# One product for two blocks of sources in an attention layer: four places of one tile instead of four tiles

## Chip, cores and metric

The kernel runs on one core of a Trainium2 chip. The metric is the device time of one execution in microseconds (us), the median over several runs. It computes a two-layer graph attention network on 1250 nodes followed by a routed feed-forward layer, all of it in one launch.

## The reference, cut to what matters

```python
def gat_layer(x, W, att_src, att_dst, bias, src, dst, heads, out_ch, concat):
    h = (x @ W.T).reshape(n, heads, out_ch)
    a_src = jnp.einsum('nhc,hc->nh', h, att_src)
    a_dst = jnp.einsum('nhc,hc->nh', h, att_dst)
    e = jax.nn.leaky_relu(a_src[src] + a_dst[dst], 0.2)
    m = jax.ops.segment_max(e, dst, num_segments=n)
    ex = jnp.exp(e - m[dst])
    denom = jax.ops.segment_sum(ex, dst, num_segments=n)
    msg = (ex / (denom[dst] + EPS))[:, :, None] * h[src]
    out = jax.ops.segment_sum(msg, dst, num_segments=n)
    ...
x = x + gnn(layernorm(x))      # layer 1: 8 heads of 128 channels, relu; layer 2: 1 head of 768
x = x + ffn(layernorm(x))
```

There are 21250 edges between 1250 nodes. An edge can occur more than once. So the sum over edges can be written with dense matrices: for a head, the weight of a pair (source, destination) is exp(e - m) times the count of edges between the two, and the sum over sources is a matrix product of these weights with the rows of h.

## The kernel before, in words

**Blocks.** The 1250 nodes are ten blocks of 125 (B = 125, NB = 10). A first stage counts edges into the tile ct, 125 x 10 x 1250 in 16-bit integers: for each place in a block (the partition) and each block s of sources, the counts for all 1250 destinations. Then comes the first attention layer, the loop over h and s at L842 to L901, which holds the change. The projection of the second layer, the second attention (L1023) and the feed-forward part follow.

**One step (h, s) of the loop.** The function weights (L636) makes the weights of head h from source block s to all 1250 destinations, in a tile pt of 125 x 1250 floats:

- L640, on VectorE (DVE), *the begin*: the larger of (row 0 + a per-source number) and row 1. The two rows belong to the head and lie in the tile rows_h, which a DMA fills for each head.
- L643, on ScalarE (ACT), *the exponential*, in place.
- L644, on DVE, *the product*: the smaller of the exponential and 1, times the counts ct[:, s].

TensorE (PE) then multiplies the ten 125 x 125 pieces of pt with the rows of h (L863) and adds into four banks of accumulators, acc. One matmul on 32-bit floats is two instructions in the profile, so a step is 20. The tile pt has four buffers (`bufs=4`), so the begin of step s waits until PE has read step s - 4.

**What else lies in the loop.**

- *The tops* (L616, called through tops and top_steps, L717 to L723): for heads 5, 6 and 7, a running maximum over one block, on DVE, ten for a head. Heads 0 to 3 have four of them each in the source, heads 4 and 5 five, head 6 four, head 7 none. From head 4 on they are queued behind the product of their step (`tc.issue_after(formed.ins)`).
- *The rows of the next head* (load_destination_rows, L621, called at s = 5): small DVE operations (L624 to L628), a transposition on PE (L582), a copy on DVE (L584), a DMA out and a DMA that spreads the rows over all partitions (L631). The begins of head h + 1 wait for this DMA.
- *The end of the head before* (take, divide, turn): ACT copies the accumulators, DVE forms reciprocals (L741, L742), ACT divides, PE transposes.
- *Matmuls that fill PE*: in heads 0 and 1 the last of the first projection (L505), from head 2 on parts of the second projection (h2_part, L810). Their results go out through ACT or, for later parts, through a DVE addition (L818).

**What sets the order.** Each engine works through its own queue in order. The library that builds the program orders each queue from the dependencies and the order of the source, with its own estimates of durations; `issue_after` adds an edge. So the order in a queue is fixed before the run, and need not be that of the source.

The second attention layer uses the same function weights with 250 destinations at a time (weights2, L951).

Of the kernel before, what the change touches and what calls it, by code (L numbers as in the profile page):

```python
# [25 lines left out]
F32 = mybir.dt.float32  # L26
# [5 lines left out]
OP = mybir.AluOpType  # L32
AX = mybir.AxisListType

N = 1250
# [7 lines left out]
B = 125  # L43
NB = N // B
# [28 lines left out]
def gnn_ffn(  # L73
# [25 lines left out]
    nc = tc.nc  # L99

    def pool(name, bufs=1, space=None, stack=ctx):
        if space is None:
            return stack.enter_context(tc.tile_pool(name=name, bufs=bufs, reuse_waits="tile"))
        return stack.enter_context(tc.tile_pool(name=name, bufs=bufs, space=space))
# [7 lines left out]
    def ps_mm(name):  # L112
        return mm_pool[0].tile([128, 512], F32, tag="mm", name=name)

    def ps_tr(name):
        return psum.tile([128, 512], F32, tag="tr", bufs=2, name=name)
# [51 lines left out]
    def half_w(i, name):  # L168
        return big.tile([128, 4 * D], F32, tag="wa" if i == 0 else "wb", name=f"{name}{i}")
# [55 lines left out]
    ct = gpool.tile([B, NB, N], U16, name="ct")  # L225
# [363 lines left out]
    def low_high(a_s, shape, name):  # L589

        lo = const.tile(shape, F32, name=f"{name}_lo")
        nc.vector.tensor_scalar(lo, a_s, SLOPE, None, op0=OP.mult)
        hi = const.tile(shape, F32, name=f"{name}_hi")
        nc.vector.tensor_scalar(hi, a_s, 1.0 - SLOPE, None, op0=OP.mult)
        return lo, hi
# [7 lines left out]
    def load_source_row(hd, sp, row, name, to=None, tag="src_row", bufs=2):  # L603

        if to is None:
            to = sp.tile([128, N], F32, tag=tag, bufs=bufs, name=f"srow_{name}")
        nc.sync.dma_start(to, row.partition_broadcast(128))
        hd.src_row = to[:B]
# [24 lines left out]
        )  # L633
        hd.rows = t[:B]

    def weights(o, hd, lo, hi, s, c0, c1):  # L636

        begun = nc.vector.scalar_tensor_tensor(  # L640
            o, hd.rows[:, 0, c0:c1], hi, hd.rows[:, 1, c0:c1], op0=OP.add, op1=OP.max
        )
        nc.scalar.activation(o, o, AF.Exp, bias=lo, scale=1.0)  # L643
        formed = nc.vector.scalar_tensor_tensor(  # L644
            o, o, 1.0, ct[:, s, c0:c1], op0=OP.min, op1=OP.mult
        )
        return begun, formed


    heads = [Head() for _ in range(H1)]  # L650
# [25 lines left out]
    for b in range(4, NB):  # L676
# [9 lines left out]
        if b == 6:  # L686
            attention_columns()
            as1_lo, as1_hi = low_high(a1[:, 0], [B, H1, NB], "as1")
# [17 lines left out]
    ap = pool("attn", stack=attn)  # L706
# [20 lines left out]
    def take(h, acc):  # L727

        sums = ap.tile([B, NB, C1 + 1], F32, tag="sums", bufs=1, name=f"sums{h}")
        for g in range(NG):  # L730
            n = min(PER, NB - g * PER)
            act_copy(
                sums[:, g * PER : g * PER + n],
                acc[g][:B, : n * (C1 + 1)].rearrange("p (j c) -> p j c", j=n),
            )
        return sums

    def divide(h, sums):

        rec = ap.tile([B, NB], F32, tag="rec", bufs=2, name=f"rec{h}")  # L740
        nc.vector.tensor_scalar(rec, sums[:, :, C1], DEN_EPS, None, op0=OP.add)  # L741
        nc.vector.reciprocal(rec, rec)  # L742
        for d in range(NB):
            nc.scalar.activation(sums[:, d, :C1], sums[:, d, :C1], AF.Copy, scale=rec[:, d : d + 1])

    def turn(h, sums, g):

        n = min(PER, NB - g * PER)
        p = ps_tr(f"h1tp{h}_{g}")
        for j in range(n):  # L750
            nc.tensor.transpose(p[:, j * B : (j + 1) * B], sums[:, g * PER + j, :C1], ident[:B, :B])
        nc.scalar.activation(
            groups[h // 4][:, h % 4, g * PER * B : (g * PER + n) * B], p[:, : n * B],
            AF.Relu, bias=b1c[:, h : h + 1], scale=1.0,
        )
# [16 lines left out]
    def fold_att2(g, w2n):  # L772
        p = ps_tr(f"v2p{g}")
        for k in range(KD):
            for j in range(4):
                nc.tensor.matmul(
                    p[32 * j : 32 * j + 2, :128], att2c[:, k], w2n[:, k, j * 128 : (j + 1) * 128],
                    start=(k == 0), stop=(k == KD - 1),
                )
        v2_row = ap.tile([2, F1 // 2], F32, tag="v2_row", bufs=1, name=f"v2_row{g}")  # L780
        for j in range(4):
            act_copy(v2_row[:, j * C1 : (j + 1) * C1], p[32 * j : 32 * j + 2, :C1])
        v2_rows.append(v2_row)
# [16 lines left out]
    def load_w2(i):  # L800
        w2h.append(half_w(i, "w2s").rearrange("p (h f) -> p h f", h=4))
        nc.sync.dma_start(
            w2h[i], w2t[i * 512 : (i + 1) * 512].rearrange("(h p) f -> p h f", p=128)
        )
# [32 lines left out]
    h2_first = [(b, g) for b in range(NB) for g in range(2)]  # L837
    begun_in = {2: (5, 7, 9), 3: (4, 6, 7, 9)}
    late = []
    load_w2(0)  # L840
    todo = None
    for h in range(H1):  # L842
        hd = heads[h]
        acc = [ps_mm(f"acc{h}_{g}") for g in range(NG)]
        for s in range(NB):
            pt = ap.tile([B, N], F32, tag="pt", bufs=4, name=f"pt{h}_{s}")
            begun, formed = weights(
                pt, hd, as1_lo[:, h, s : s + 1], as1_hi[:, h, s : s + 1], s, 0, N
            )
            if s in top_steps.get(h, ()):  # L850
                if h < 4:
                    tops.pop(0)()
                else:
                    with tc.issue_after(formed.ins):
                        tops.pop(0)()
            if s == 0 and todo is not None:
                sums = take(*todo)
            if s == 1 and todo is not None:
                with tc.issue_after(begun.ins):
                    divide(todo[0], sums)  # L860
            for d in range(NB):
                g, j = divmod(d, PER)
                summed = nc.tensor.matmul(  # L863
                    acc[g][:B, j * (C1 + 1) : (j + 1) * (C1 + 1)],
                    pt[:, d * B : (d + 1) * B], h1v[h // 4][:, h % 4, s, :],
                    start=(s == 0 and j == 0), stop=(s == NB - 1), skip_group_check=True,
                )
            if s in (2, 3) and todo is not None:
                with tc.issue_after(summed.ins):
                    for g in (2 * s - 4, 2 * s - 3):  # L870
                        turn(todo[0], sums, g)
            if h in (4, 5) and s == 4:
                with tc.issue_after(formed.ins), tc.issue_after(summed.ins):
                    fold_att2(h - 4, w2n)
            if h in (4, 5) and s == 6:
                with tc.issue_after(formed.ins), tc.issue_after(summed.ins):
                    turn_att2(h - 4)
            if s == 5 and h + 1 < H1:
                load_destination_rows(heads[h + 1], ap, a1[:, 1, h + 1], f"h{h + 1}", 2)
            if s == 0 and h == 3:  # L880
                load_source_row(heads[7], ap, as1_d[7], "h7")
            if s in begun_in.get(h, ()):
                late.append((h2_first.pop(0), range(h, 4)))
                h2_part(0, *late[-1][0], range(h))
            if 4 <= h < H1 - 1 and s in ((2, 4, 6, 8) if h < 6 else (2, 5, 8)):
                h2_part(0, *h2_first.pop(0))
            if h == H1 - 1 and s in (1, 2, 3, 4, 5, 7, 8):
                at, hs = late.pop(0)
                h2_part(0, *at, hs)
            if h == H1 - 1 and s == 6:  # L890
                attention2(range(H1 - 1))
            if fill and s in (2, 4, 5, 7):
                fill.pop(0)()
        if h == 1:
            h2.append(big.tile([B, NB, D + 1], F32, tag="t", name="h2"))
            nc.gpsimd.memset(h2[0][:, :, D : D + 1], 1.0)
        if h in (3, 4):
            w2n = load_w2n(h - 3)
        if h == 5:
            load_w2(1)  # L900
        todo = h, acc  # L901
# [25 lines left out]
    as2_lo, as2_hi = low_high(a2[:, :, 0], [B, NB], "as2")  # L927
    hd = Head()
# [20 lines left out]
    pt2 = []  # L949

    def weights2(q):  # L951
        pt2.append(sp.tile([B, NB, 2 * B], F32, tag="pt2", bufs=3, name=f"pt2_{q}"))
        for s in range(NB):
            weights(
                pt2[q][:, s], hd, as2_lo[:, s : s + 1], as2_hi[:, s : s + 1], s,
                2 * q * B, 2 * (q + 1) * B,
            )

    for b in range(NB):
        for g in range(2):  # L960
# [62 lines left out]
    for q in range(NB // 2):  # L1023
        pt = pt2[q]
# [147 lines left out]
    pt = ps_tr("hidt")  # L1172
# [4 lines left out]
    pt = ps_tr("hidt4")  # L1177
# [15 lines left out]
    for r1, r0 in ((0, 3), (1, 4), (2, None)):  # L1193
        pair = [(1, r1)] if r0 is None else [(1, r1), (0, r0)]
        for m in range(KH):
            for r, a in pair:
                for g in range(2):
                    q = 32 * (2 * (1 - r) + g)
# [6 lines left out]
    for r in range(2):  # L1205
        for g in range(2):
            q = 32 * (2 * (1 - r) + g)
# [68 lines left out]
```

## Time and profile before

| | |
|---|---|
| median of 3 runs | 735.99 us (734.98 to 737.64) |
| the profiled execution | 735.11 us, its span 733.1 us |
| granted TensorE clock, mean | 0.993 |
| busy in the span | PE 95%, DVE 76%, ACT 40%, POOL 13% |
| L640 in the first layer | 80 of 125x1250, 118.6 us, 1511 ns each |
| L643 in the first layer | 80 of 125x1250, 105.7 us, 1336 ns each |
| L644 in the first layer | 80 of 125x1250, 114.7 us, 1452 ns each |
| L863, PE | 1600 instructions, 188.5 us |
| L616, DVE, all | 90, 130.7 us |

The span runs from the first to the last instruction that the profiler shows; the time of the execution has 2.0 us around it. The mean duration of an instruction (the column "mean ns") is longer than its step in a full queue, because the next one starts before the last is written off; the timeline gives the steps. "Idle before" is how long the engine stood still just ahead of an instruction, and the name behind the arrow is what ended that.

### The profile page before, as it was taken

How to read it: one execution, taken by the hardware profiler on the slowest of the kernel's cores; microseconds unless marked ns; L12 is line 12 of the kernel's file. 1: busy time of each engine (PE TensorE's matmuls, PEld its weight loads, DVE VectorE, ACT ScalarE, POOL GpSimd, SP SyncE). 2: the span in 40 equal slices, each digit the busy share in tenths (PEclk: the TensorE clock that was granted, in tenths of full speed). 3: DMA queues.
4: the chain of work that ended last, by engine and by line, in shares of the span. 5: the costliest groups of instructions: out<-in, count | busy, mean ns of one | idle time of the engine just before them, and what ended most of it. 6: DMA issues, size and time to landing. Idle time of an engine off the chain costs nothing.

```text
span 733.1 us, 10360 instructions
## 1 busy us (share of the span) xinstructions
PE 698.1 (95%) x4136; PEld 535.2 (73%) x4136; DVE 553.5 (76%) x943; ACT 289.9 (40%) x502; POOL 91.7 (13%) x95
## 2 busy tenths in 40 slices
PE   3899999999999989999999899999999999999997
PEld 3767888889898878888888776555555555676755
DVE  7989999889999999999999961879487222423212
ACT  5969621143563764847474734015044000010100
POOL 8449200000000000000000000000011010023110
PEclk9899999999999999999999999999999999999999
DMA  8445000340205012040401004022110100285711
GB/s 235 165 150 202 1 0 1 124 141 1 72 1 192 10 62 70 2 157 1 157 1 71 1 23 138 5 72 65 30 34 21 41 23 21 84 276 166 283 43 43
DMA packets 21701, 58.41 MB, mean 80 GB/s; under 512 B 2414, under 2 KB 7906, under 8 KB 20498
## 3 DMA queue, kind: packets, MB, share of 16 engines
q1 hardware_dynamic: 21598, 57.68, 23.7%
q8 instruction: 33, 0.54, 0.3%
q14 instruction: 18, 0.15, 0.1%
q10 hardware_dynamic: 52, 0.04, 0.0%
HBM read 53.74 MB, written 3.98 MB: 79 GB/s over the span
## 4 chain that ended last, share of the span: by engine, by line
PE 57%; DVE 33%; DMA 5%; issue 3%; ACT 1%; SPq 0%; DVEq 0%; ACTq 0%
PE acc L1033 16%; DVE pt L640 12%; DVE pt L644 10%; PE h2p L810 9%; PE h1p L505 8%; DVE unused L616 6%; PE f L1098 5%; PE f L1082 5%; PE acc L863 5%; DMA rows_h<-r_h_d 3%; PE count L302 3%; DVE ring L242 2%; PE xtp L397 1%; DMA r_h_d<-r_h_s 1%; PE xt2p L397 1%
## 5 line engine op out<-in xcount | busy, mean ns | idle before, releaser
L863 PEld LDWEIGHTS acc<-g,pt 125*125 125x125 f32 x1600 | 184.3, 189 | 25.5 <-DVE pt L644 18.5
L863 PE MATMUL acc<-g,pt 125*125 125x129 f32 x1600 | 188.5, 276 | 11.9 <-DVE pt L644 11.7
L643 ACT ACTIVATE pt<-pt,as_lo 125x1250 f32<-125x1250 f32 (+1 forms) x130 | 127.3, 1012 | 127.4 <-DVE pt L640 126.7
L644 DVE SCALAR_TENSOR_TENSOR pt<-pt,ct 125x1250 f32<-125x1250 f32 (+1 forms) x130 | 133.0, 1051 | 0.8 <-ACT pt L643 0.6
L1033 PE MATMUL acc<-h,pt 125*125 125x385 f32 (+1 forms) x400 | 129.7, 486 | 0.0
L640 DVE SCALAR_TENSOR_TENSOR pt<-rows_h,as_hi 125x1250 f32<-125x1250 f32 x80 | 118.6, 1511 | 2.3 <-DMA rows_h<-r_h_d 2.3
L1033 PEld LDWEIGHTS acc<-h,pt 125*125 125x125 f32 x400 | 74.6, 187 | 53.9
L810 PE MATMUL h2p<-w2s,g 128*125 128x384 f32 x320 | 110.7, 488 | 0.0
L505 PE MATMUL h1p<-w1s,xt 128*125 128x256 f32 x480 | 107.0, 380 | 0.8 <-ACT g L401 0.8
L505 PEld LDWEIGHTS h1p<-w1s,xt 128*125 128x125 f32 x480 | 88.9, 188 | 14.0 <-ACT g L401 1.2
L810 PEld LDWEIGHTS h2p<-w2s,g 128*125 128x125 f32 x320 | 56.9, 188 | 33.5 <-issue 1.2
L1029 POOL TENSOR_TENSOR xb<-xb,b2r 125x768 f32<-125x768 f32 x10 | 18.1, 1809 | 368.2 <-DMA xb<-in_x 368.2
L616 DVE CUSTOM_DVE_ANT_0 unused<-rows,absent 125x1250 bf16<-125x1250 f32 x40 | 58.3, 1459 | 2.4 <-ACTq L695 1.1
L616 DVE CUSTOM_DVE_ANT_0 unused<-srow_h,absent 125x1250 bf16<-125x1250 f32 x40 | 57.9, 1448 | 0.3
L285 POOL TENSOR_SCALAR at<-node,place 125x125 bf16<-125x125 f16 x60 | 52.2, 887 | 19.9 <-PE count L302 17.0
L1102 DVE TENSOR_TENSOR o<-f,o 125x384 f32<-125x384 f32 x20 | 11.1, 557 | 52.5 <-PE f L1098 28.2
L242 DVE TENSOR_SCALAR ring<-node,key 125x420 bf16<-125x420 f16 x158 | 45.1, 347 | 2.7 <-PE count L302 2.7
L302 PE MATMUL count<-ring,places 125*125 125x420 bf16 (+27 forms) x192 | 29.5, 290 | 13.2 <-DVE ring L242 13.2
L401 ACT ACTIVATE g<-h1p 125x256 f32<-125x256 f32 x40 | 15.3, 382 | 66.2 <-PE h1p L505 66.2
L1098 PE MATMUL f<-wf,gt 128*125 128x384 f32 x120 | 39.5, 486 | 0.0
L302 PEld LDWEIGHTS <-places 125*125 125x125 bf16 x192 | 22.2, 148 | 15.7 <-DVE places L260 8.6
L1098 PEld LDWEIGHTS f<-wf,gt 128*125 128x125 f32 x120 | 22.5, 188 | 15.1
(190 smaller groups left out, 580.9 us busy)
## 6 DMA issues: line engine op xcount, KB each, us to landing
rows_h<-r_h_d SPq DMA_DIRECT2D x8, 1250.0 KB
w_more<-in_atom_in_t SPq DMA_DIRECT2D x3, 1152.0 KB
w_more<-in_atom_out_t SPq DMA_DIRECT2D x3, 1152.0 KB
x<-in_x SPq DMA_DIRECT2D x10, 336.0 KB
xb<-in_x SPq DMA_DIRECT2D x10, 336.0 KB
srow_h<-as_d SPq DMA_DIRECT2D x5, 625.0 KB
w1n<-in_w SPq DMA_DIRECT2D x2, 1536.0 KB
w1s<-in_w1t SPq DMA_DIRECT2D x2, 1536.0 KB
```

The lines of the kernel that those rows point to most:

```text
L242: return nc.vector.tensor_scalar(t, nodes, col, None, op0=OP.is_equal)
L285: nc.gpsimd.tensor_scalar(at, node[:, :B], place[:, c : c + 1], None, op0=OP.is_equal)
L302: newest["count"] = nc.tensor.matmul(banks[k][:B, SB * (d0 - AREA * k) : SB * (d1 - AREA * k)], at, by[:, SB * (d0 - f) : SB * (d1 - f)], ...
L505: newest["h1"] = nc.tensor.matmul(p[:B, :256], xt[:, k, b * B : (b + 1) * B], w1s[g][:, k, i * 256 : (i + 1) * 256], start=(k == 0), stop= ...
L616: nc.vector.tensor_tensor_reduce(out=unused, in0=hd.src_row, in1=absent[:, b], scale=1.0, scalar=-ABSENT, op0=OP.subtract, op1=OP.max, acc ...
L640: begun = nc.vector.scalar_tensor_tensor(o, hd.rows[:, 0, c0:c1], hi, hd.rows[:, 1, c0:c1], op0=OP.add, op1=OP.max)
L643: nc.scalar.activation(o, o, AF.Exp, bias=lo, scale=1.0)
L644: formed = nc.vector.scalar_tensor_tensor(o, o, 1.0, ct[:, s, c0:c1], op0=OP.min, op1=OP.mult)
L810: nc.tensor.matmul(p[:B, :384], groups[i][:, h, b * B : (b + 1) * B], w2h[i][:, h, g * 384 : (g + 1) * 384], start=(h == hs[0]), stop=(h = ...
L863: summed = nc.tensor.matmul(acc[g][:B, j * (C1 + 1) : (j + 1) * (C1 + 1)], pt[:, d * B : (d + 1) * B], h1v[h // 4][:, h % 4, s, :], start= ...
L1033: nc.tensor.matmul(acc[g][:B, : c1 - c0], pt[:, s, i * B : (i + 1) * B], h2[:, s, c0:c1], start=(s == 0), stop=(s == NB - 1),)
L1098: nc.tensor.matmul(p[:B, :384], gt[:, m, i, :], wf2[:, m, c], start=(m == 0), stop=(m == KH - 1),)
```

## The change

The function weights is split in two. begin_weights does the begin and the exponential of one step; form_weights does the product of n neighbouring steps in one DVE instruction. In the first layer the four buffers of pt become four places of one tile, exps (125 x 4 x 1250). Steps are taken in pairs, an even s with the next odd one: two begins, two exponentials, and then one product of 125 x 2500 over two neighbouring places and two neighbouring blocks of ct. Only the first two steps of head 0 keep a product each. That leaves 39 products of two steps and 2 of one, where there were 80. The name formed, behind which the tops of heads 4 to 6 are queued, is now the product of the pair; begun, behind which divide is queued, is the begin of the pair's first step. The second layer keeps its 50 products of 125 x 250.

```diff
-    def weights(o, hd, lo, hi, s, c0, c1):
+    def begin_weights(o, hd, lo, hi, c0, c1):
         begun = nc.vector.scalar_tensor_tensor(
             o, hd.rows[:, 0, c0:c1], hi, hd.rows[:, 1, c0:c1], op0=OP.add, op1=OP.max
         )
         nc.scalar.activation(o, o, AF.Exp, bias=lo, scale=1.0)
-        formed = nc.vector.scalar_tensor_tensor(
-            o, o, 1.0, ct[:, s, c0:c1], op0=OP.min, op1=OP.mult
-        )
-        return begun, formed
+        return begun
+
+    def form_weights(o, s, n, c0, c1):
+        return nc.vector.scalar_tensor_tensor(
+            o, o, 1.0, ct[:, s : s + n, c0:c1], op0=OP.min, op1=OP.mult
+        )
...
+    exps = ap.tile([B, 4, N], F32, name="exps")
...
         for s in range(NB):
-            pt = ap.tile([B, N], F32, tag="pt", bufs=4, name=f"pt{h}_{s}")
-            begun, formed = weights(
-                pt, hd, as1_lo[:, h, s : s + 1], as1_hi[:, h, s : s + 1], s, 0, N
-            )
+            at = (NB * h + s) % 4
+            pt = exps[:, at]
+            many = 1 if (h, s) in ((0, 0), (0, 1)) else 2 - s % 2 * 2
+            if many:
+                parts = [
+                    begin_weights(
+                        exps[:, at + i], hd, as1_lo[:, h, s + i : s + i + 1],
+                        as1_hi[:, h, s + i : s + i + 1], 0, N,
+                    )
+                    for i in range(many)
+                ]
+                begun = parts[0]
+                formed = form_weights(exps[:, at : at + many], s, many, 0, N)
...
     def weights2(q):
...
-            weights(
-                pt2[q][:, s], hd, as2_lo[:, s : s + 1], as2_hi[:, s : s + 1], s,
+            begin_weights(
+                pt2[q][:, s], hd, as2_lo[:, s : s + 1], as2_hi[:, s : s + 1],
                 2 * q * B, 2 * (q + 1) * B,
             )
+            form_weights(pt2[q][:, s : s + 1], s, 1, 2 * q * B, 2 * (q + 1) * B)
```

## The prediction, made before the changed kernel was run

> **What bounds the kernel now.** I read the page first, to see which engine the stage of the change hangs on.
>
> ```profile
> PE 698.1 (95%) x4136; PEld 535.2 (73%) x4136; DVE 553.5 (76%) x943; ACT 289.9 (40%) x502; POOL 91.7 (13%) x95
> ```
>
> Over the whole span PE looks like the bound, but a share is a mean over stages. So I cut the first attention layer (156.7 to about 442 us) into four stretches: heads 0 and 1, heads 2 and 3, heads 4 to 6, head 7. The columns are the stretch, its length, and the busy time of each engine.
>
> ```profile
> 157.00:229.00 72.00, 70.35 (x511) 66.17 (x510) 72.00 (x69) 37.59 (x51) 0.12 (x1) 1.00 0.13 46
> 229.00:290.00 61.00, 54.83 (x426) 50.16 (x426) 60.37 (x58) 38.96 (x61) 0.00 (x0) 0.97 0.19 64
> 290.00:403.00 113.00, 111.56 (x873) 94.70 (x872) 111.66 (x117) 65.89 (x106) 0.00 (x0) 1.00 0.20 72
> 403.00:452.00 49.00, 46.29 (x355) 36.45 (x354) 32.84 (x33) 27.17 (x50) 0.00 (x0) 1.00 0.07 21
> ```
>
> From 157 to 403 us DVE (third) is idle for 2.0 of 246 us, and PE (first) for 9.3. DVE is the bound and PE stands right behind it. In the last 49 us it is the other way round: PE 46.3, DVE 32.8. The chain of waits agrees: 10% of the span is on L644 and 12% on L640, nearly all before 408 us; behind that it runs on PE. So up to 403 us each us less on DVE counts and each us of new DVE idle time counts too; behind that DVE counts only where PE waits for it.
>
> The prices come from the groups of instructions kept apart by shape (busy, mean ns, idle before):
>
> ```profile
> L640 DVE SCALAR_TENSOR_TENSOR pt<-rows_h,as_hi 125x1250 f32<-125x1250 f32 x80 | 118.6, 1511 | 2.3 <-DMA rows_h<-r_h_d 2.3
> L644 DVE SCALAR_TENSOR_TENSOR pt<-pt,ct 125x1250 f32<-125x1250 f32 x80 | 114.7, 1452 | 0.8 <-ACT pt L643 0.6
> L643 ACT ACTIVATE pt<-pt,as_lo 125x1250 f32<-125x1250 f32 x80 | 105.7, 1336 | 50.7 <-DVE pt L640 50.0
> ```
>
> DVE waited for an exponential for 0.6 us in all 80 steps. How the order manages that is in DVE's timeline, first where there are tops, then where there are none:
>
> ```profile
> 174.89 2.95 DVE L640 SCALAR_TENSOR_TENSOR pt<-rows_h,as_hi 125x1250 f32<-125x1250 f32 x2
> 177.75 1.46 DVE L616 CUSTOM_DVE_ANT_0 unused<-srow_h,absent 125x1250 bf16<-125x1250 f32 x1
> 179.13 0.09 DVE L616 DVE_READ_ACCUMULATOR2_ANT top<- 125x1 f32 x1
> 179.13 2.83 DVE L644 SCALAR_TENSOR_TENSOR pt<-pt,ct 125x1250 f32<-125x1250 f32 x2
> ...
> 245.69 1.51 DVE L640 SCALAR_TENSOR_TENSOR pt<-rows_h,as_hi 125x1250 f32<-125x1250 f32 x1
> 247.12 1.45 DVE L644 SCALAR_TENSOR_TENSOR pt<-pt,ct 125x1250 f32<-125x1250 f32 x1
> 248.50 1.51 DVE L640 SCALAR_TENSOR_TENSOR pt<-rows_h,as_hi 125x1250 f32<-125x1250 f32 x1
> 249.93 1.45 DVE L644 SCALAR_TENSOR_TENSOR pt<-pt,ct 125x1250 f32<-125x1250 f32 x1
> ```
>
> In the first stretch two begins are followed by a top and then two products: the pairs are there already. In the second a begin and a product alternate; the product there belongs to an earlier step, and covers the exponential of the begin just issued. The starts give the steps of a full queue: a begin 1.43 us (245.69 to 247.12), a product 1.37 to 1.38, a top 1.38 (177.75 to 179.13). ACT's timeline gives the delay: its two exponentials from 176.44 end at 179.21, and the second begin ended at 177.84. So a product can start about 1.4 us after the begin of its own step.
>
> **The change, part by part.**
>
> *The saving.* In the second layer seven products of 250 columns take 2.30 us of the chain, 0.329 each, and one of 1250 takes 1.37. That is (1.37 - 0.329)/1000 = 1.041 ns a column and 0.069 us fixed. A pair is 2500 x 1.041 + 69 ns = 2.67 us against 2.74: 0.07 saved, 39 times. 34 of the pairs lie in heads 0 to 6, where DVE bounds: 34 x 0.069 = **-2.35 us**. The five of head 7 lie beside PE. The Trainium skill (VectorE: DVE Perf Modes, "The DRAIN you can't avoid") says that a flush of about the duration less 266 ns follows every operation, and advises fewer operations; at 266 ns fixed, 34 joined products would give 9 us. The row has 69 ns, and the row decides.
>
> *The new wait.* The joined product needs both exponentials, the second 1.4 us after the second begin ends. Today the first product of the two (1.37), or a product of another step, lies there; that cover is gone. Queued behind the waiting product are the begins of the next pair, and PE waits for those. A top (1.38) closes the gap, to 0.02. Heads 0 to 6 have 34 pairs and 30 tops. In heads 4 and 5 the pair (0,1) gets none, because the pair (2,3) has two; in head 6 the pairs (6,7) and (8,9) get none; in heads 0 to 3, 16 tops go to 19 pairs. That leaves seven pairs with no top. What else fits there is the begin of the pair after next, if its place is free: PE reads 2.2 us from a place (20 instructions take 2.20 us of the chain). Worked from the end of a product at 0: second begin 0 to 1.43; the place free at about 2.4; next begin 2.4 to 3.83; product to 6.50. Two begins and two products are 5.60 now, so this pair loses 0.9. Waiting for the exponential instead gives two pairs in 12.63 against 11.20, 0.7 each. The ends are 0 and the whole delay, 1.40 - 0.07 = 1.33; I take 0.8, the row of PE's step being the nearest: 7 x 0.8 = **+5.6 us** (0 to 9.3).
>
> *The start of head 7.* PE waited 2.71 us for its first product, which ended 4.30 + 1.37 us after the rows landed (402.61). The joined one ends 4.30 + 2.67 after them, and PE is the bound from there: **+1.3 us**.
>
> *The rows of head 7.* The last top of head 6 (at 387.75) stands behind the product of step 4, in future behind that of steps 4 and 5, which ends 1.3 later. The rows come from this top, with other DVE work between that can move behind: 0 to 1.3, I take **+0.6**.
>
> *Inside head 7* no top is left. A pair's loop there is begin 1.43, delay 1.4, product 2.67, together 5.5; PE has 4.4 of steps and at least 1.3 of other matmuls beside it in most pairs. **+0.5** (0 to 1).
>
> *The heads before.* PE also gets the first product of heads 1 to 6 later by 1.3. There it has matmuls of its own to put in front (2.75 us of L810 at 331.53), or the slack of heads 2 and 3: 0, upper end 6 x 1.3 = 7.8.
>
> *The tile and the second layer.* Four places wait place by place, as the ring of 20 places at L273 does now, whose writes run 17 in a row while PE reads other places; the same depth as four buffers. The second layer's 50 products keep their shape. Nothing for either, and no DMA is moved by itself.
>
> Sum: -2.35 + 5.6 + 1.3 + 0.6 + 0.5 = +5.65 us on the profiled 735.11, 740.8. The median stands 0.9 above that execution: **741.6 us**. The best case is the saving alone, -2.7 with head 7's share; all upper ends give -2.35 + 9.3 + 1.3 + 1.3 + 1 + 7.8 = +18.4.
>
> A rule on both sides: the Trainium skill (Perfetto Trace Analysis, "Optimizing Scalar/DVE Operations") advises larger operations where an engine is saturated, and breaking instructions up where it is not but causes bubbles on others. By the row of stretches the first half holds to 403 us, and the second in head 7 speaks against the change. It gives no price for the wait between, on which my sum turns.
>
> **The rivals.**
>
> 1. *Faster: the order finds cover for every pair.* The planner places begins of the next pair, or tops, between the second begin and the product throughout. It decides as soon as 1.4 us of ready work lies in each of the 34 gaps. For it: DVE's order now has nearly no wait, tops may go anywhere in heads 0 to 3, and single begins can fill. Against: four places are two pairs, so that a begin of the next but one waits for PE. Price: -2.7 us, or by mean durations (2 x 1452 - (2604 + 150) ns, 39 times) -5.9: 733.3, down to 730. Chance 0.25.
> 2. *No change:* half the gaps covered and head 7 late by 1 us; saving and loss meet. 736. Chance 0.15.
> 3. *Much slower:* tops are placed where they cover nothing, and the wait is paid by nearly every pair: 34 x 0.8 gives +25, 39 x 1.33 gives +52: 761 to 788. The tops of heads 4 to 6 stand behind the product and not before it, which speaks for it; that a begin then follows speaks against. Chance 0.09. That the one tile is followed as a whole, so that a pair's begins wait for PE's last read of all four places (about 4 us for each pair, over 150 us), has 0.01; the ring speaks against it.
>
> **How the numbers follow.** My forecast, a loss of 2.2 to 16 us, has 0.50; its own range is 738.2 to 752. A measurement of this kernel tells about 0.3%, 2.2 us, from no change. Faster than 733.8 is rival 1, 0.25; within 2.2 us is rival 2, 0.15; slower is the forecast and rival 3, 0.60. The range 732.5 to 752 leaves out rival 3 (0.10) and the better half of rival 1 (0.1).
>
> **What would show it.** Right: 39 products of 125x2500 of about 2.75 us mean and 2.67 us step; idle time of DVE before them, ended by the exponential, 5 to 8 us in all and in few pairs; DVE busy less by 3 to 6 us; PE waiting longer than 2.71 for head 7's first product. Wrong: that idle time under 2 us (rival 1), or over 20 us in most pairs (rival 3); a product step far from 2.67; or a loss that lies behind 452 us, where I expect none.

## The result, and the profile after

The changed kernel takes 762.88 us (median of 4 runs) against 735.49 us before in the same runs: a ratio of 1.0358, 95% interval 1.0325 to 1.039. It is slower by some 27 us. The forecast was a loss of 5.6 us with a range up to 752, so the sign was right and the size was wrong, by a factor of five. In what follows a ratio always stands against the kernel before, run on the same chip.

The profiled execution has a span of 759.9 us, 26.8 more. Busy times, granted clock and the chain of waits on the page after:

```profile
PE 707.7 (93%) x4136; PEld 544.0 (72%) x4136; DVE 552.7 (73%) x904; ACT 292.1 (38%) x502; POOL 91.9 (12%) x95
PEclk9899999999999989999999899999999999999999
PE 67%; DVE 22%; DMA 4%; issue 4%; ACT 2%; SPq 0%; ACTq 0%
```

Two things stand out. PE is busy for 9.6 us *more* with the same 4136 instructions (698.1 before). And the chain has moved to PE: 67% of the span, 57% before. The groups by shape say more (busy, mean ns, idle before; the line numbers have moved: L876 was L863, L639 was L640, L648 was L644):

```profile
L876 PE MATMUL acc<-g,exps 125*125 125x129 f32 x1600 | 197.3, 284 | 28.9 <-DVE exps L648 24.8 <-DVE rec L744 4.1
L639 DVE SCALAR_TENSOR_TENSOR exps<-rows_h,as_hi 125x1250 f32<-125x1250 f32 x80 | 119.6, 1514 | 21.6 <-PE acc L876 15.8 <-DMA rows_h<-r_h_d 5.6
L648 DVE SCALAR_TENSOR_TENSOR exps<-exps,ct 125x2500 f32<-125x2500 f32 x39 | 107.5, 2758 | 8.9 <-ACT exps L642 8.8
```

The first line holds the loss. Ahead of the aggregation matmuls PE stood still for 28.9 us, against 11.9 before (the same group there, 11.7 of it for the product). That is 17.0 us of new waiting; with the 9.6 us of longer work it makes 26.6, nearly the whole of the 26.8. The 4.1 us put down to a reciprocal (L744) are one wait, at 238.58: DVE began that reciprocal at 238.34, when the joined product was done. The new idle time on DVE has three main sorts: 15.8 us for places that PE had not read yet (nothing before), 8.8 us for the exponential (0.6 before), 5.6 us for the rows (2.3 before).

The same four stretches as before, the last one longer because the layer ends later:

```profile
157.00:229.00 72.00, 69.56 (x502) 64.69 (x501) 71.90 (x61) 37.51 (x50) 0.00 (x0) 1.00 0.13 46
229.00:290.00 61.00, 50.06 (x359) 46.12 (x358) 55.32 (x49) 35.15 (x55) 0.12 (x1) 0.92 0.17 58
290.00:403.00 113.00, 104.12 (x799) 89.30 (x798) 97.84 (x82) 62.06 (x102) 0.00 (x0) 0.97 0.19 63
403.00:470.00 67.00, 60.32 (x466) 51.61 (x465) 50.27 (x43) 30.50 (x44) 0.00 (x0) 0.95 0.08 26
```

In the first stretch DVE stays full, 71.90 of 72 us. From 229 us on both engines have holes at once, DVE 5.7 of 61 and 15.2 of 113, PE 10.9 and 8.9. Neither is the bound any more; they wait for each other. And the granted clock (the column behind the five engines) falls to 0.92 to 0.97, where before only the second stretch had 0.97.

DVE's timeline shows both sides of the pairs, first one with a top, then one without:

```profile
172.44 1.52 DVE L639 SCALAR_TENSOR_TENSOR exps<-rows_h,as_hi 125x1250 f32<-125x1250 f32 x1
173.87 1.46 DVE L616 CUSTOM_DVE_ANT_0 unused<-srow_h,absent 125x1250 bf16<-125x1250 f32 x1
175.25 0.09 DVE L616 DVE_READ_ACCUMULATOR2_ANT top<- 125x1 f32 x1
175.26 1.52 DVE L639 SCALAR_TENSOR_TENSOR exps<-rows_h,as_hi 125x1250 f32<-125x1250 f32 x1
176.70 2.76 DVE L648 SCALAR_TENSOR_TENSOR exps<-exps,ct 125x2500 f32<-125x2500 f32 x1
...
297.65 1.50 DVE L639 SCALAR_TENSOR_TENSOR exps<-rows_h,as_hi 125x1250 f32<-125x1250 f32 x1
300.56 2.76 DVE L648 SCALAR_TENSOR_TENSOR exps<-exps,ct 125x2500 f32<-125x2500 f32 x1 [1.41 <-ACT exps L642]
```

In the first part the second begin already belongs to the next pair, so the exponential is covered and nothing is lost, 6.9 us from product to product as before. In the second part nothing lies between, and DVE waits 1.41 us. Only eight such waits came, 8.8 us: they are not the main loss.

**Where in a head it is lost.** The time from a head's first aggregation step on PE to that of the next, worked out from the starts of the groups of 200 such matmuls in PE's timeline (head 7: to its own end):

| head | 0 | 1 | 2 | 3 | 4 | 5 | 6 | 7 |
|---|---|---|---|---|---|---|---|---|
| before | 34.3 | 35.3 | 32.7 | 32.6 | 36.5 | 36.4 | 35.7 | 33.8 |
| after | 35.4 | 38.1 | 34.5 | 40.6 | 40.0 | 39.2 | 40.0 | 36.1 |

The sums differ by 26.5 us: nearly all of the loss lies in this loop. A wait ahead of a head's first step counts here for the head before. Ahead of the first steps of heads 1 to 7 PE waited 20.5 us in all, 9.0 before; the other waits in this group grew by 5.4. First the kernel before (heads 1, 2 and 3; head 7 had 2.71), then after (heads 2, 4, 5 and 7; head 1 had 2.25 and head 6, shown below, 2.40):

```profile
199.14 6.87 PE L863 MATMUL acc<-g,pt 125*125 125x129 f32 x60 [1.65 <-DVE pt L644]
234.47 4.67 PE L863 MATMUL acc<-g,pt 125*125 125x129 f32 x40 [1.40 <-DVE pt L644]
267.16 8.43 PE L863 MATMUL acc<-g,pt 125*125 125x129 f32 x60 [3.20 <-DVE pt L644]
```

```profile
238.58 6.30 PE L876 MATMUL acc<-g,exps 125*125 125x129 f32 x40 [4.05 <-DVE rec L744]
313.63 8.53 PE L876 MATMUL acc<-g,exps 125*125 125x129 f32 x60 [3.65 <-DVE exps L648]
353.62 4.67 PE L876 MATMUL acc<-g,exps 125*125 125x129 f32 x40 [2.40 <-DVE exps L648]
432.81 7.00 PE L876 MATMUL acc<-g,exps 125*125 125x129 f32 x40 [5.78 <-DVE exps L648]
```

Head 3 lost most, 8.0 us, and part of that not at a head's start: PE waited 3.51 us ahead of its third step, and the next 20 instructions took 4.13 us instead of 2.37. DVE's queue has four begins there between the first joined product and the next two:

```profile
269.65 2.76 DVE L648 SCALAR_TENSOR_TENSOR exps<-exps,ct 125x2500 f32<-125x2500 f32 x1
280.89 5.44 DVE L648 SCALAR_TENSOR_TENSOR exps<-exps,ct 125x2500 f32<-125x2500 f32 x2 [0.75 <-ACT exps L642]
283.70 4.13 PE L876 MATMUL acc<-g,exps 125*125 125x129 f32 x20 [3.51 <-DVE exps L648]
```

That order came with the plan of this kernel. It is kept in tops_early below; half_exp has its like in head 2 (3.60 us of waiting). In head_start, rows_early and warm it is gone, and PE's wait at this place is 0.85 us or nothing. So up to some 5 us (3.51 and the 1.76 behind it) of what those three runs gave back may be this order and not their edit.

What happens at a boundary is seen at the start of head 6. First the kernel before, then after (start, duration, idle time ahead in brackets):

```profile
366.64 1.52 DVE L640 SCALAR_TENSOR_TENSOR pt<-rows_h,as_hi 125x1250 f32<-125x1250 f32 x1 [0.69 <-DMA rows_h<-r_h_d]
370.52 4.57 PE L863 MATMUL acc<-g,pt 125*125 125x129 f32 x40
370.88 1.45 DVE L644 SCALAR_TENSOR_TENSOR pt<-pt,ct 125x1250 f32<-125x1250 f32 x1
```

```profile
384.89 4.39 DVE L639 SCALAR_TENSOR_TENSOR exps<-rows_h,as_hi 125x1250 f32<-125x1250 f32 x3 [0.70 <-DMA rows_h<-r_h_d]
388.05 2.37 PE L876 MATMUL acc<-g,exps 125*125 125x129 f32 x20
390.00 2.77 DVE L648 SCALAR_TENSOR_TENSOR exps<-exps,ct 125x2500 f32<-125x2500 f32 x1 [0.72 <-ACT exps L642]
392.82 6.33 PE L876 MATMUL acc<-g,exps 125*125 125x129 f32 x40 [2.40 <-DVE exps L648]
```

Before, the first product of head 6 was done 5.6 us after its rows had landed (366.64 to 370.88 + 1.37), while PE was still at the last step of head 5: PE went through both without a gap (40 instructions in 4.57). After, it takes 7.8 us (384.89 to 392.68, where the next instruction starts): begin, begin and a third begin, the rest of the second exponential (on ACT, 0.72 us of waiting), and a product of double length. PE ends head 5 at 390.4 and waits 2.40 us, where the kernel before had 0.5 us to spare (product done at 372.25, PE's first step of head 6 at 372.72). Then its 40 instructions take 6.33 us instead of 4.57: the clock is halved. The windows around it show that (the first number behind the five engines is the granted clock):

```profile
389.80:393.20 3.40, 1.00 (x9) 0.81 (x8) 3.20 (x2) 2.71 (x6) 0.00 (x0) 1.00 0.00 0
393.30:396.60 3.30, 3.30 (x18) 3.30 (x17) 2.48 (x5) 0.91 (x1) 0.00 (x0) 0.50 0.00 0
```

At head 5 the kernel before had as little room. The 40 instructions below are the last step of head 4 and, from 336.31, the first of head 5, whose product was done at 336.04:

```profile
331.53 2.75 PE L810 MATMUL h2p<-w2s,g 128*125 128x384 f32 x8
334.11 4.57 PE L863 MATMUL acc<-g,pt 125*125 125x129 f32 x40
334.67 1.46 DVE L644 SCALAR_TENSOR_TENSOR pt<-pt,ct 125x1250 f32<-125x1250 f32 x1
```

### The profile page after: what moved, and what is told of

The parts are those of the page before. It is cut to its first block, busy times and chain, and to the rows that moved or that the text cites. A ratio compares the mean times of both kernels' runs of the same rounds, so it can differ in the third digit from the quotient of the medians.

```text
span 759.9 us, 10330 instructions
## 1 busy us (share of the span) xinstructions
PE 707.7 (93%) x4136; PEld 544.0 (72%) x4136; DVE 552.7 (73%) x904; ACT 292.1 (38%) x502; POOL 91.9 (12%) x95
## 4 chain that ended last, share of the span: by engine, by line
PE 67%; DVE 22%; DMA 4%; issue 4%; ACT 2%; SPq 0%; ACTq 0%
PE acc L1047 16%; PE acc L876 13%; PE h2p L813 11%; DVE exps L648 8%; PE h1p L505 7%; DVE exps L639 7%; PE f L1112 5%; PE f L1096 5%; DVE unused L616 5%; PE count L302 2%; DMA x<-in_x 2%; DMA bal<-in_balance 1%; DVE ring L242 1%; DMA rows_h<-r_h_d 1%; PE xt2p L397 1%
## 5 line engine op out<-in xcount | busy, mean ns | idle before, releaser
L876 PE MATMUL acc<-g,exps 125*125 125x129 f32 x1600 | 197.3, 284 | 28.9 <-DVE exps L648 24.8
L876 PEld LDWEIGHTS acc<-g,exps 125*125 125x125 f32 x1600 | 192.7, 197 | 40.9 <-DVE exps L648 31.5
L642 ACT ACTIVATE exps<-exps,as_lo 125x1250 f32<-125x1250 f32 x80 | 106.5, 1337 | 83.8 <-DVE exps L639 80.0
L639 DVE SCALAR_TENSOR_TENSOR exps<-rows_h,as_hi 125x1250 f32<-125x1250 f32 x80 | 119.6, 1514 | 21.6 <-PE acc L876 15.8
L648 DVE SCALAR_TENSOR_TENSOR exps<-exps,ct 125x2500 f32<-125x2500 f32 (+1 forms) x41 | 110.3, 2695 | 8.9 <-ACT exps L642 8.8
L813 PEld LDWEIGHTS h2p<-w2s,g 128*125 128x125 f32 x320 | 57.4, 188 | 35.7 <-issue 1.2
L642 ACT ACTIVATE pt<-pt,as_lo 125x250 f32<-125x250 f32 x50 | 21.6, 493 | 76.7 <-DVE pt L639 76.7
```

The costliest lines, as they stand in the source:

```text
L639: begun = nc.vector.scalar_tensor_tensor(o, hd.rows[:, 0, c0:c1], hi, hd.rows[:, 1, c0:c1], op0=OP.add, op1=OP.max)
L648: return nc.vector.scalar_tensor_tensor(o, o, 1.0, ct[:, s : s + n, c0:c1], op0=OP.min, op1=OP.mult)
L813: nc.tensor.matmul(p[:B, :384], groups[i][:, h, b * B : (b + 1) * B], w2h[i][:, h, g * 384 : (g + 1) * 384], start=(h == hs[0]), stop=(h = ...
L876: summed = nc.tensor.matmul(acc[g][:B, j * (C1 + 1) : (j + 1) * (C1 + 1)], pt[:, d * B : (d + 1) * B], h1v[h // 4][:, h % 4, s, :], start= ...
```

## The experiments

Theories: **A**, the joined product itself withholds the first step of a pair; in its wide form it loses in every pair. **B**, the order of the queue. **C**, the wait for the exponential in pairs that no top covers, which was my recorded reason. **D**, the one tile. **E**, the start of a head: a loop from step 5 on PE over the rows, begins, exponential and product back to PE. **F**, PE's clock. **G**, depth: four places are only two pairs. Each kernel below was timed in three rounds.

### Which part of the change: the product alone

*One product for each step, all else as changed (split).*

```diff
-                formed = form_weights(exps[:, at : at + many], s, many, 0, N)
+                for i in range(many):
+                    formed = form_weights(exps[:, at + i : at + i + 1], s + i, 1, 0, N)
```

> The changed kernel with its one tile and its pairs of begins, but with a product of 125x1250 for each step instead of one of 125x2500 for two. Theory A (the joined product itself: it holds the first step of a pair back from PE until the second is ready, and with four places only two such pairs are in flight): nearly all of the 27 us comes back, 734 to 739 us. Theory B (the order of the queue, two begins ahead of the products, is what costs): stays above 750 us. Theory C (waits for the exponential in pairs without a top): some 9 us comes back, the DVE idle time that the exponential ended in the changed kernel, so about 754.

Measured: 737.68 us, ratio 1.0006 (0.9987 to 1.0024). All of the loss is gone. Its groups:

```profile
L877 PE MATMUL acc<-g,exps 125*125 125x129 f32 x1600 | 190.0, 278 | 12.3 <-DVE exps L648 12.2
L648 DVE SCALAR_TENSOR_TENSOR exps<-exps,ct 125x1250 f32<-125x1250 f32 x80 | 114.0, 1448 | 0.1
```

PE's wait is back at 12.3 us and DVE's wait for the exponential at 0.1. Two begins still stand ahead of two products in this run's queue, so B falls, and the joining of the product is the cause.

*The tile alone (tile_only): `many = 1` for every step.*

> The four places of one tile, but every step with its own begin, exponential and product, as before the change. Theories A, B and C: as before the change, 734 to 738 us. Theory D (the one tile is followed as a whole, or its places wait longer than four buffers): slow like the changed kernel, over 750 us.

Measured: 737.19 us, ratio 1.0006 (0.9983 to 1.003). D falls: four places of one tile cost what four buffers do.

### Is it the exponential?

*The tops of heads 4 to 6 ahead of the product (tops_early).*

```diff
-                    with tc.issue_after(formed.ins):
+                    with tc.issue_after(parts[-1].ins):
                         tops.pop(0)()
```

> The changed kernel with the tops of heads 4 to 6 queued behind the begin of the pair's second step, so that they can lie ahead of the joined product and cover the exponential. Theory C: DVE's idle time ended by the exponential falls from 8.9 to under 4 us and the time by 4 to 8 us, to about 756. Theory A: the idle time moves, the product comes later for PE, and the time stays within 4 us of 763 or gets longer.

Measured: 759.56 us, ratio 1.0319 (1.0283 to 1.0354), some 3 us back, with intervals that overlap. In heads 4 and 5 the tops now lie ahead of the product. DVE's wait for the exponential hardly moved in sum (8.3 us), and the wait for rows grew from 5.6 to 10.4. That is what A expected. But since the wait moved and did not go, this run alone does not exclude C.

*The exponential over 625 of the 1250 destinations (half_exp).*

```diff
-        nc.scalar.activation(o, o, AF.Exp, bias=lo, scale=1.0)
+        e = o[:, : (c1 - c0) // 2] if c1 - c0 == N else o
+        nc.scalar.activation(e, e, AF.Exp, bias=lo, scale=1.0)
```

> The changed kernel with the first layer's exponential over the first 625 of 1250 destinations only, so that its delay falls from 1.34 to some 0.75 us; the other destinations keep what the begin left, so this kernel leaves out part of the computation. Theory C (the wait of the joined product for the second exponential is most of the loss): 0.6 us for each of about 20 pairs that wait and for 7 head starts, 15 us and more, under 750 us. Theory E (the loop from the rows to PE's first step, in which the exponential is one of four parts): 0.6 us for 7 heads and a few windows, 5 to 8 us, 754 to 758.

Measured: 754.97 us, ratio 1.0228 (1.0195 to 1.0261). Between 9 and 10 us back by the ratios, near E's 5 to 8 and short of C's 15. DVE still waited 9.3 us for the exponential; the planner, which knows the shorter duration, had ordered the queues anew, so this run alone does not decide it.

### The start of a head, and the rows

*A product a step for the first two steps of every head (head_start).*

```diff
-            many = 1 if (h, s) in ((0, 0), (0, 1)) else 2 - s % 2 * 2
+            many = 1 if s < 2 else 2 - s % 2 * 2
```

> The changed kernel with a product for each of the first two steps of every head (before: of head 0 alone), 32 joined products instead of 39. Theory E (the loss is that PE starves at the start of each head, and its clock is halved behind that): 10 to 18 us comes back, 745 to 753 us, with PE's waits of over 2 us and the half-clock windows gone. Theory A in its wide form (the loss is spread over all pairs): 7 of 39 of it, about 5 us, so about 758.

Measured: 747.18 us, ratio 1.0151 (1.0117 to 1.0186). With 7 of the 39 joined products undone, 15 of the 27 us come back, 0.0207 of 0.0358. PE's wait falls from 28.9 to 16.7 us. That is E's range and three times what the wide form of A expected, and it stays well above it without the 5 us of head 3's order. E had also expected waits over 2 us and half-clock stretches to go; three such waits (2.20, 2.25 and 3.25 us) and four of seven stretches are left.

*The rows of the next head asked for at step 3 instead of 5 (rows_early), in the changed kernel.*

```diff
-            if s == 5 and h + 1 < H1:
+            if s == (5 if h == 6 else 3) and h + 1 < H1:
```

> The changed kernel with the rows of the next head asked for at step 3 instead of 5 (head 6 stays at 5, since the tops of head 7 end at its step 4). Theory E (the start of a head hangs on a loop: step 5 on PE, rows, two begins, exponential, joined product): rows come some 6 us earlier, DVE no longer waits for them, PE's waits at the starts of heads 1 to 6 shrink, 745 to 752 us. Theory G (places, not rows, hold back the begins): within 4 us of 763.

Measured: 744.14 us, ratio 1.0098 (1.0072 to 1.0124). Nearly three quarters of the loss is gone, with every product joined. Its groups:

```profile
L876 PE MATMUL acc<-g,exps 125*125 125x129 f32 x1600 | 192.2, 279 | 16.8 <-DVE exps L648 16.4
L639 DVE SCALAR_TENSOR_TENSOR exps<-rows_h,as_hi 125x1250 f32<-125x1250 f32 x80 | 119.6, 1512 | 12.3 <-PE acc L876 7.3 <-DMA rows_h<-r_h_d 4.9
```

PE's wait fell by 12.1 us and its busy time in this group by 5.1. With the rows there early, DVE can begin the next head while PE is still busy with the last, so the longer way through a joined product is hidden: PE's waits ahead of heads 5 and 6, 2.40 us each, are gone. Head 7, whose rows were not early, keeps its gap: 5.84 us of PE's wait is ahead of its first step.

*The same edit in the kernel before (rows_early_before).*

> The kernel before the change with the rows of the next head asked for at step 3 instead of 5. Its waits for rows were 2.3 us in all: 732 to 737 us under every theory; under theory E a few tenths of a per cent faster.

Measured: 732.96 us, ratio 0.9955 (0.9932 to 0.9979). By the ratio it is some 3 us ahead of the kernel before, the fastest of the study with rows_all_single below (their intervals overlap): the loop bounded the kernel before a little, too.

*Both edits in the changed kernel (rows_and_start).*

> The changed kernel with rows asked for at step 3 (head 6: at 5) and a product for each of the first two steps of every head. Theory E: both shorten the same path from the rows to PE's first step, so they add only in part: 737 to 741 us, against 744 and 747 with one of them. If they were two separate losses (18.7 and 15.7 us), the sum would bring it to 729.

Measured: 738.96 us, ratio 1.0033 (1.0016 to 1.0051). They add only in part, as E says: two edits on one path.

### The clock

*Twelve matmuls on a constant ahead of the first step of heads 1 to 7 (warm).*

```diff
+            if h > 0 and s == 0:
+                with tc.issue_after(summed.ins):
+                    warm = ps_tr(f"warm{h}")
+                    for i in range(12):
+                        nc.tensor.matmul(warm[:, :128], ident, ident, start=True, stop=True)
             for d in range(NB):
```

> The changed kernel with twelve extra 128x128 matmuls on a constant (about 2.6 us of PE, result unused) in PE's queue ahead of the first step of heads 1 to 7, where PE stands still. Theory F (a part of the loss is PE's clock, halved for 3.4 us at a time after such a wait, seven times instead of once): the half-clock windows fall to two or fewer, 1.7 us comes back for each, 750 to 756 us. Theory A alone (the wait itself is the loss): no gain, or up to 3 us lost where the extra matmuls outlast the wait, 761 to 766 us.

Measured: 756.54 us, ratio 1.0259 (1.0229 to 1.0288): the changed kernel with *more* work on PE is faster by 0.0099, 7 us. The record of the granted clock has seven stretches of 3.41 us at half in the first layer after the change, one before, three in this run; four fewer at 1.7 us each are 6.8, the expected size. (The number differs between executions of one kernel; the mean granted clock was 0.983 to 0.993 before and 0.974 to 0.979 after.) But the table of heads puts the gain elsewhere. In the profiled executions the loop is 3.7 us shorter; heads 2 and 3, where DVE's order also changed, are shorter by 4.7, and the other six longer by 1.0. So the clock's part in the 7 us is not shown. What is read directly is that PE needed 9.6 us more for the same instructions after the change. The aggregation matmuls in this run:

```profile
L881 PE MATMUL acc<-g,exps 125*125 125x129 f32 x1600 | 191.4, 278 | 12.7 <-DVE exps L648 10.3 <-DVE rec L744 2.4
```

*The same with early rows (rows_early_warm).*

> The joined kernel with rows asked for at step 3 and the twelve extra matmuls ahead of the first step of heads 1 to 7. With early rows there were four half-clock windows in the first layer, two of them at head 7. If the clock is part of what is left: 738 to 741 us against 744. If PE's waits are now too short for it, the extra matmuls cost what they take beyond the waits: 744 to 750.

Measured: 750.95 us, ratio 1.0189 (1.0165 to 1.0212). Here the matmuls cost 7 us. Where PE hardly waits they are only work; with early rows nothing is to be had from the clock this way, though the half-clock stretches fell from four to two.

### Depth

*Three buffers instead of four in the kernel before (bufs3).*

> The kernel before the change with three buffers of pt instead of four. Theory G (what the joined product costs is depth: four places hold only two units): a loss of its own, 739 to 750 us, in waits of DVE for PE. Theory E or F alone: a buffer less changes little, under 739 us.

Measured: 739.09 us, ratio 1.003 (1.0011 to 1.005). DVE's wait for PE's reads rose from nothing to 5.6 us, yet only 2 us were lost, at the edge between the two expectations: depth matters little where a unit is one step.

*All rows early (step 1; for head 7 at step 4, with the tops of head 6 one step ahead), joined products (rows_all_joined), and the same with a product for each step (rows_all_single).*

```diff
-            if s == 5 and h + 1 < H1:
+            if s == (4 if h == 6 else 1) and h + 1 < H1:
...
-    top_steps |= {4: (2, 3, 5, 6, 8), 5: (2, 3, 5, 6, 8), 6: (1, 2, 3, 4)}
+    top_steps |= {4: (2, 3, 5, 6, 8), 5: (2, 3, 5, 6, 8), 6: (0, 1, 2, 3)}
```

> The changed kernel, all products joined as it has them, with rows asked for at step 1 and, for head 7, at step 4 of head 6, whose tops move one step ahead (0 to 3 instead of 1 to 4). Theory E: the last long gap of the run with early rows, 43 us between the first begins of heads 6 and 7 against 35 in the other kernel, closes by some 5 us: 736 to 741 us. Theory A in its wide form, that the pairs lose inside the heads too: 742 us or more.

> The kernel before the change with the same early rows and tops: the best order found so far with a product for each step. 729 to 734 us. Set beside the joined one of this call it gives the price of joining once the start of a head is off the path: theory E has them within 6 us of each other, theory A in its wide form 10 us or more apart.

Measured: 743.92 us, ratio 1.0092 (1.0067 to 1.0117), and 734.18 us, ratio 0.9966 (0.9949 to 0.9983). For the first, E's expectation (736 to 741) missed and A's (742 or more) came. Against the run with step 3 the wait for rows fell from 4.9 to 1.6 us, and heads 3 and 6 got shorter (34.9 to 32.0 and 38.7 to 36.4 us), but heads 1 and 2 got longer by as much (33.8 to 36.7 and 35.4 to 38.0): DVE now waits 8.7 us for places and 6.6 us for the exponential. So with the rows early, joining still costs 9 to 10 us. That is beyond E's 6 and just short of A's 10: a third of the loss does not go with the start of a head.

*Six places instead of four, all rows early (rows_all_six_places); the rows kept as 16-bit floats to make room.*

```diff
-    exps = ap.tile([B, 4, N], F32, name="exps")
+    exps = ap.tile([B, 6, N], F32, name="exps")
...
-            at = (NB * h + s) % 4
+            at = (NB * h + s) % 6
```

> As the joined kernel with all rows early, but with six places instead of four, that is three pairs in flight. To make room, the head's rows are kept as 16-bit floats, which rounds the weights and halves the rows' DMA. Theory G (depth): the rest of the loss goes, the saving of 0.07 us a pair shows, 728 to 733 us, and DVE waits for PE's reads under 2 us. If the exponential is what is left: little change, within 3 us of the joined one with four places, DVE's waits for it still 5 us or more.

Measured: 737.67 us, ratio 1.0008 (0.9989 to 1.0028).

*The control: 16-bit rows and four places (rows_all_four_bf).*

> The control of the run with six places: all rows early, joined products, the head's rows as 16-bit floats (which rounds the weights), but four places. If depth gave the 6 us: 742 to 745 us, as with 32-bit rows. If the shorter DMA gave it: 736 to 739.

Measured: 742.96 us, ratio 1.0071 (1.0049 to 1.0093), so most of the gain is not the shorter DMA's. The begin and the product, first with six places, then the begin of the control:

```profile
L639 DVE SCALAR_TENSOR_TENSOR exps<-rows_h,as_hi 125x1250 f32<-125x1250 bf16 x80 | 119.2, 1508 | 2.4 <-DMA rows_h<-r_h_d 2.4
L648 DVE SCALAR_TENSOR_TENSOR exps<-exps,ct 125x2500 f32<-125x2500 f32 x39 | 107.2, 2748 | 3.6 <-ACT exps L642 3.6
```

```profile
L639 DVE SCALAR_TENSOR_TENSOR exps<-rows_h,as_hi 125x1250 f32<-125x1250 bf16 x80 | 120.0, 1513 | 10.7 <-PE acc L876 8.5 <-DMA rows_h<-r_h_d 2.2
```

With three pairs in flight no begin waits for PE any more (8.5 us in the control), and the wait for the exponential is 3.6 us, 6.6 in the control. The gain over the control is 0.0063 of the ratio, 4.6 us, and the time stays above the 728 to 733 us that G expected. Nor is all of it shown to be depth: in the control four begins and a top lie between two products of head 2, PE waits 4.15 us behind them, and with six places that order is gone. Even then the joined kernel is not faster than a product a step (0.9966): about 3 us remain, near the 3.6 us of waiting that is left, though that was not tried by itself.

## Why the prediction was wrong

**The cause.** Joining makes the unit that passes between DVE and PE twice as large. The way from a head's rows to its first product grows by 2.2 us (5.6 to 7.8 at head 6), and the rows themselves are asked for behind step 5 on PE, so the growth comes back to PE. Heads 4 to 6, whose begins waited for the rows (1.76, 1.78 and 0.70 us), had 0.1 to 0.5 us of slack before, from the end of the first product to PE's first step. At heads 1, 2 and 7 the begins did not wait for rows; there PE waited for the first product before, and the longer one came later still. Behind most of these waits lies a stretch of 3.4 us at half clock. That all of it is the joined product is shown by split; that most of it goes with the start of a head and the rows, by head_start and rows_early (over half and nearly three quarters, less up to 5 us each for the order in head 3). The clock's part, 9.6 us of longer work, is read from the profile and was not isolated by a run. About 9 to 10 us stay once the rows are early; about half of that came back with six places. How it divides between depth, the exponential and the order of the queue is open.

Step by step, against the sum on record:

- *The saving*: right in size. Two joined products in a row take 5.44 us with a mean of 2.76, so a step is 2.68 (forecast 2.67), and 0.07 us a pair is saved. The products' busy time fell by 4.4 us (114.7 to 107.5 + 2.8), but DVE's as a whole only by 0.8, not by 3 to 6.
- *The new wait*, +5.6: the mechanism and the size were near. DVE waited 8.8 us for the exponential, in 8 waits.
- *The heads before*, taken as 0 with an upper end of 7.8: **this step failed.** PE's waits ahead of the first steps of heads 1 to 6 went from 6.25 to 14.75 us, by 8.5. The step argued that PE has matmuls of its own to put ahead of a first product that comes 1.3 us later. The row it cited (2.75 us of L810 at 331.53) was already spent there: in the kernel before PE worked without a gap through it into head 5's first step, which began 0.3 us after its product was done (336.31 and 336.04). A filler that is in use is no reserve. Nor was there slack at heads 1 to 3, where PE waited 1.65, 1.40 and 3.20 us already. What was late was 2.2 us and not 1.3, for the first product also needs the second begin and its exponential, and the loop through the rows was not followed at all: I looked at the rows only for head 7.
- *The start of head 7*, +1.3: its first step on PE waited 5.78 us, against 2.71 before, so +3.1, and at half clock for 6.8 us behind it.
- *The rows of head 7*, +0.6, and *inside head 7*, +0.5: its first begin waited 3.25 us for a place that PE had not read, not for its rows. Head 7 itself took 2.3 us more (36.1 against 33.8); the half clock in its first 40 instructions (7.00 us instead of 4.57) is as much.
- *The tile*, nothing: right for the tile, wrong for "the same depth". Counted in bytes the depth is the same; counted in units it is two instead of four, and DVE waited 15.8 us for places. My hand-worked cycle of a pair had PE start a pair at once; it did not allow for PE being late.
- *The clock* was no term of the sum, and PE's longer work is 9.6 us: **the other step that failed.** The profile before showed one such case: 3.20 us of waiting at 267.16, and then 60 instructions in 8.43 us, which took 6.77 at 164.84.
- *The rivals*: the measured time lies at the lower end of "much slower" (761), but not by its mechanism. It had the exponential's wait paid by nearly every pair; the wait was 8.8 us, and the run with the tops ahead of the product gave back 3 us only.

So the loss of 26.6 us on PE is 8.5 at heads 1 to 6 (forecast 0), 3.1 at head 7 (1.3), 5.4 of waits inside the heads, and 9.6 of longer work (no term). That the sign came out right is in part luck: most of the loss lies in terms that the sum had at 0 or not at all.

The rule of the Trainium skill that spoke against the change (Perfetto Trace Analysis, "Optimizing Scalar/DVE Operations": break instructions up where an engine is not saturated but causes bubbles on others) turned out to bear on heads 2 to 6 too, not only on head 7: after the change DVE was no longer full from 229 us on (55.32 of 61 us), and PE's wait for the product went from 11.7 to 24.8 us.

## What to carry to other kernels

Where two engines are both close to full and hand work to each other, the size of the unit can count more than the fixed cost of an instruction: here joining two operations saved 0.07 us a time, 2.7 in all, and cost ten times that. Before joining, follow each loop that comes back to the consumer (here over a DMA once a head), add the longer unit to its length, and look whether the consumer had any gap there; count buffers in units, not in bytes. Look also where the planner's order puts the longer unit (head 3 here). And where a step waits for a transfer that could be asked for earlier, try that first: it hid most of this loss, and it made the kernel before faster too (0.9955).

## What the runs showed of the hardware

A wait of PE can cost some 1.8 us more behind it: 40 matmul instructions took 6.33 us instead of 4.57 after 2.40 us of waiting. Another wait of the same 2.40 us, at 353.62, cost nothing (4.67 us). In the record of the granted clock after the change, the half-clock stretches of the first layer last 3.41 us or twice that, and their starts (239.65, 266.95, 284.02, 314.74, 393.25 and 430.79) lie whole multiples of 3.413 us apart: a fixed grid. At 392.8 the wait lay within one step, in which PE was busy for 1.00 us. On the same grid the wait at 353.62 fell into two steps:

```profile
348.90:352.20 3.30, 2.32 (x21) 2.13 (x19) 2.39 (x2) 3.14 (x7) 0.00 (x0) 1.00 0.00 0
352.30:355.70 3.40, 2.08 (x18) 2.08 (x19) 2.90 (x4) 1.60 (x2) 0.00 (x0) 1.00 0.00 0
```

PE was busy for over 2 us in each, and the clock stayed at 1.00 (until 393.25). The Trainium skill (TensorE: Matmul & The Clock Gate, "Part 1: The HAM clock gate (the "warmup" mystery)") states a free-running window of 3413 ns and half clock behind an idle one; the length and the grid agree with the record here. That a window need not be wholly idle, 1.00 us of work in it not being enough, is this case's row.
